# The D term of a selective scan: from matmuls on TensorE to a ScalarE write into the accumulator bank, with the convolution and the filler moved between slots

## The chip, the core and the metric

The kernel runs on one core of one Trainium2 chip. Its time is the device time of one execution in microseconds (us). Before the change the median of three executions was 8080.22 us. A profile is one execution recorded by the hardware profiler. In it PE is TensorE (PEld its weight loads), DVE is VectorE, ACT is ScalarE, POOL is GpSimd and SP is the queue that issues most DMAs.

## The reference, cut to what matters

The input has shape (4, 512, 64, 64): 4 batches, 512 channels, 4096 positions. Layer 0 is group norm, LayerNorm over channels, a Mamba block applied to four chunks of 128 channels with shared weights, a skip, a second LayerNorm and a 512 x 512 projection. Layer 1 is group norm and a linear attention with 8 heads. Each layer is added to its input. For a chunk x of shape (L, 128) the Mamba block computes

```python
xi, z = split(x @ in_proj_w.T)               # 256 inner channels each
xc = silu(causal_conv4(xi) + conv_b)
dt, Bs, Cs = split(xc @ x_proj_w.T)          # 8, 16 and 16 columns
dt = softplus(dt @ dt_proj_w.T + dt_proj_b)
h  = exp(dt * A) * h + (dt * xc) * Bs        # for each channel and 16 states, along L
y  = sum_over_states(h * Cs) + xc * D_param  # the last product is the D term
out = (y * silu(z)) @ out_proj_w.T + skip_scale * x
```

The change concerns `xc * D_param`, and the places at which the next chunk's `causal_conv4` and `z` are computed.

## The kernel before

**Steps and slots.** One step handles one batch b, one tile t of 512 positions and one chunk c of 128 channels: 4 x 8 x 4 = 128 steps. A step has 16 slots (`SLOTS`), 2048 slots in all. Slots 0 to 7 belong to inner channels 0 to 127 (e = 0), slots 8 to 15 to inner channels 128 to 255 (e = 1). Two slots together handle one group of 4 states; each slot does half of it. All emission is written out by hand under a manual schedule, so every engine executes its instructions in the order in which the Python code emits them.

**What a slot holds** (`slot`, L659). VectorE runs two scans (L673), called scan(s,0) and scan(s,1) here for slot s. Each scan takes its decay factors from a PSUM bank dA and its inputs from bx. ScalarE writes each dA bank with an exponential (`decay`, L642); there are three such banks, so it runs at most three scans ahead: decay(k), with k = 2s + i within the step, is queued behind scan number k - 3 and what that slot emitted before it. GpSimd makes bx two slots ahead (`drive`, L651, operation L655). After an odd slot it also stores the last state (L683) and multiplies the last quarter of the positions by C (L684). VectorE multiplies the other three quarters by C in `product` (L696), which is called product(s) here. It reads C from a single PSUM bank, c_all.

**Where C comes from.** `c_row` (L636) is one bf16 matmul that spreads the C rows of one group over the partitions. It is emitted inside `product` of an odd slot, when the bank has been read for the last time. c_all(s), for an even s, is the matmul that slot s's product reads. Behind it TensorE gets the fold of the group just finished (`fold_states`, L702): four matmuls of 32 columns each that run side by side and add the group's states into PSUM bank y. There is one bank for y. Because `AWAY = (3, 10)`, in which wide VectorE operations may follow the scans, product(s) runs after the first scan of slot s + 1, except for s = 4 and s = 11, whose products run at the end of their own slot. So slot 4 holds product(3), then one scan, then product(4).

**What else is emitted in each slot** (`after`, inside the loop over s from L1046). Pieces of the step's own bookkeeping have fixed slots:

- slot 0: `take_y` of the step before (e = 1), a ScalarE copy of bank y; slot 8: the same for this step (e = 0). It overwrites xc in `xz` with y.
- slots 1 and 9: the product with the gate on GpSimd; slot 2: `time_banks` (L544), two matmuls into two work banks; slot 3: `time_steps` (L551), the softplus on ScalarE that empties them, between two loads of activation tables; slot 4: dt times xc on GpSimd and `out_proj` (L724); slot 6: `with_skip`; slot 10: silu of the step after next, again between two table loads.
- slots 3, 5, 6, 7, 8, 9: one piece each of `inputs` (L512) of the step after next: two convolution taps, two taps, two taps, two taps, gate matmul, gate matmul. Each bank is copied out by ScalarE one slot later.

Everything else is filler that comes from three queues (`ahead`, `late`, `rest`): the LayerNorms (wide VectorE operations of 2.26 us only in slots 3 and 10), the projection, and the attention of the batch before. A filler piece is begun if there is credit for TensorE work (counted in fp32 matmuls of 512 columns) and if `room` finds fewer than `limit[0]` fillers holding a bank. There are three work banks (`ps_w`) for all of these.

**The D term.** At the first fold of each half step, bank y is started by `diagonal`: four matmuls of 32 x 32, side by side, of `dg` (D on a diagonal) with xc. The same helper starts the bank of `out_proj` with the skip scale.

The records of all matmuls stand at one line of the profile, L124, since one helper issues them.

## Time and profile before

| quantity | value |
|---|---|
| executions before (median, lowest, highest) | 8080.22, 8074.53, 8089.37 us |
| profiled execution, its own time | 8087.92 us |
| its span, first to last instruction | 8086.2 us |
| scans (L673) | 4096, mean 1267 ns (3584 of them), 1206 ns (512 of them) |
| products (L696) | 2048, mean 931 ns |
| exponentials (L647) | 4096, mean 688 ns |
| D packs (y<-xz,dg) | 2048 records, two to a matmul, 340.4 us busy |
| table loads | 1283 ns each |
| mean granted TensorE clock | 0.888 |

A row of the profile gives line, engine, operation, result and operands, shapes and count, and then the busy time and mean duration. In a timeline row the first number is the start in us, the second the duration of the rows merged in it. A bracket at its end tells how long the engine had been idle before the row and what ended that wait. In the view of waits a row gives who waited for whom, the total in us, how often, and the longest. Idle time of an engine is worth removing only if that engine sets the end.

### The profile page before, as it was taken

How to read it: one execution, taken by the hardware profiler on the slowest of the kernel's cores; microseconds unless marked ns; L12 is line 12 of the kernel's file. 1: busy time of each engine (PE TensorE's matmuls, PEld its weight loads, DVE VectorE, ACT ScalarE, POOL GpSimd, SP SyncE). 2: the span in 40 equal slices, each digit the busy share in tenths (PEclk: the TensorE clock that was granted, in tenths of full speed). 3: DMA queues.
4: the chain of work that ended last, by engine and by line, in shares of the span. 5: the costliest groups of instructions: out<-in, count | busy, mean ns of one | idle time of the engine just before them, and what ended most of it. 6: DMA issues, size and time to landing. Idle time of an engine off the chain costs nothing.

```text
span 8086.2 us, 92449 instructions
## 1 busy us (share of the span) xinstructions
PE 6471.4 (80%) x24800; PEld 2115.5 (26%) x24800; DVE 7113.0 (88%) x6815; ACT 5514.5 (68%) x8289; POOL 6890.3 (85%) x4597
## 2 busy tenths in 40 slices
PE   5677777667788878888788888888788888888599
PEld 1111111112222222322222222332222222322144
DVE  5999999999999999899999999999999999998600
ACT  4667777777767777677776767667777777776421
POOL 4999999999989989899998989888999999889600
PEclk8787888788899989898899999899889999999699
DMA  5666666666666666676666666667666666676402
GB/s 160 166 166 160 156 147 153 157 157 166 167 167 156 162 153 156 168 188 176 169 155 164 166 165 155 155 171 187 163 158 160 156 157 152 150 194 176 110 32 89
DMA packets 829199, 1265.98 MB, mean 157 GB/s; under 512 B 183912, under 2 KB 317560, under 8 KB 816384
## 3 DMA queue, kind: packets, MB, share of 16 engines
q1 hardware_dynamic: 804736, 1222.32, 59.7%
q0 software_dynamic: 16896, 33.56, 2.4%
q10 hardware_dynamic: 7040, 4.20, 0.2%
q8 instruction: 194, 3.18, 0.2%
q14 instruction: 333, 2.73, 0.1%
HBM read 1052.78 MB, written 206.57 MB: 156 GB/s over the span
## 4 chain that ended last, share of the span: by engine, by line
DVE 22%; PE 19%; DMA 17%; POOL 14%; issue 10%; ACT 9%; SPq 8%; POOLq 0%; DVEq 0%; ACTq 0%
DVE h L673 14%; POOL bx L655 10%; DMA d_all<-d_rows 9%; DVE h L696 7%; PE pq L124 5%; SPq L622 5%; DMA b_all<-b_rows 4%; ACT dA L647 3%; PE pc L124 3%; PE pr L124 3%; SPq L572 3%; PE y L124 3%; POOL h L684 2%; PE pp L124 1%; DMA c_sb<-c_rows 1%
## 5 line engine op out<-in xcount | busy, mean ns | idle before, releaser
L655 POOL TENSOR_TENSOR bx<-d_all,b_all 128x1024 f32<-128x1024 f32 x2048 | 4817.4, 2371 | 66.9 <-DVE h L673 51.5
L673 DVE TENSOR_TENSOR_SCAN h<-dA,st,bx 128x512 f32<-128x512 f32 x3584 | 4420.5, 1267 | 80.6 <-ACT dA L647 75.4
L647 ACT ACTIVATE dA<-d_all,a_t 128x512 f32<-128x512 f32 x4096 | 2780.4, 688 | 1764.2 <-DVE h L673 1727.5
L696 DVE TENSOR_TENSOR h<-h,c_all 128x768 f32<-128x768 f32 x2048 | 1906.7, 931 | 307.5 <-PE c_all L124 298.2
L124 PE MATMUL y<-h,fold 128*32 128x512 f32 x8192 | 1280.6, 701 | 160.5 <-POOL h L684 156.1
L684 POOL TENSOR_TENSOR h<-h,c_sb 128x512 f32<-128x512 f32 x1024 | 1299.3, 1269 | 121.4 <-DMA c_sb<-c_rows 33.5
L124 PE MATMUL pc<-xn,w_cv 128*128 128x512 f32 x2048 | 1078.8, 662 | 178.2 <-DVE xn L410 116.7
L124 PE MATMUL c_all<-parts,sel 128*128 128x384 bf16 x1024 | 368.3, 360 | 1058.5 <-DVE h L696 1056.1
L124 PE MATMUL pq<-w_qk,xa 128*128 128x512 f32 x2048 | 990.7, 615 | 1.9 <-ACT xa L348 1.9
L673 DVE TENSOR_TENSOR_SCAN h<-dA,bx 128x512 f32<-128x512 f32 x512 | 601.2, 1206 | 58.8 <-ACT dA L647 54.6
L124 PEld LDWEIGHTS pc<-xn,w_cv 128*128 128x128 f32 x2048 | 395.9, 204 | 807.7 <-issue 445.6
L124 PEld LDWEIGHTS <-sel 128*128 128x128 bf16 x1280 | 127.5, 100 | 1724.4 <-DVE h L696 1495.6
L683 POOL COPY st<-h 128x4 f32<-128x4 f32 x1024 | 206.9, 202 | 425.2 <-DVE h L673 382.2
L124 PEld LDWEIGHTS pq<-w_qk,xa 128*128 128x128 f32 x2048 | 402.8, 199 | 468.7 <-issue 446.2
L124 PE MATMUL pr<-xb,m 128*128 128x512 f32 x1024 | 500.4, 626 | 24.8 <-DMA xb<-x 16.5
L124 PE MATMUL pp<-xn,w_pr 128*128 128x512 f32 x1024 | 487.6, 602 | 3.8 <-DVE xn L410 3.8
L124 PEld LDWEIGHTS y<-h,fold 128*32 128x32 f32 x8192 | 170.9, 114 | 743.6 <-issue 281.0
L124 PE MATMUL y<-xz,dg 32*32 32x512 f32 x2048 | 340.4, 741 | 0.0
L720 POOL TENSOR_TENSOR xz<-xz 128x512 f32<-128x512 f32 x256 | 325.4, 1271 | 2.7 <-ACT xz L717 2.7
L561 POOL TENSOR_TENSOR dt<-dt,xz 128x1024 f32<-128x1024 f32 x128 | 302.2, 2361 | 25.5 <-ACT dt L553 25.5
L124 PE MATMUL pd<-xz,w_xp 128*128 128x512 f32 x512 | 311.6, 740 | 7.8 <-ACT xz L987 7.8
L771 ACT ACTIVATE kq<-pq 128x512 f32<-128x512 f32 x256 | 150.6, 588 | 232.6 <-PE pq L124 230.5
(169 smaller groups left out, 6063.9 us busy)
## 6 DMA issues: line engine op xcount, KB each, us to landing
d_all<-d_rows SPq DMA_DIRECT2D x2048, 256.0 KB, 6.6
b_all<-b_rows SPq DMA_DIRECT2D x4096, 64.0 KB, 2.2
d_rows<-dt SPq DMA_DIRECT2D x256, 512.0 KB, 3.7
c_sb<-c_rows SPq DMA_DIRECT2D x4096, 16.0 KB, 1.9
xs<-in_x_dram SPq DMA_DIRECT2D x32, 1024.0 KB, 5.8
xn<-in_x_dram SPq DMA_DIRECT2D x32, 1024.0 KB, 5.7
xr<-in_x_dram POOLq DMA_DIRECT2D x32, 1024.0 KB, 11.2
x<-xr SPq DMA_DIRECT2D x32, 1024.0 KB, 4.3
```

The source lines that it names most:

```text
L124: nc.tensor.matmul(out_, lhsT, rhs, **how)
L561: nc.gpsimd.tensor_tensor(f["both"][:, 1], f["both"][:, 0], f["xz"][:, 0], ALU.mult)
L572: nc.sync.dma_start(d[k * BLK : (k + 1) * BLK, v], src)
L622: nc.sync.dma_start(dst[k * BLK : (k + 1) * BLK, :], rows_[q * KS + k, :].partition_broadcast(BLK))
L647: nc.scalar.activation(dAs[k], fs[n]["d_all", e][:, 0, j, :], AF.Exp, scale=a_t[:, e, j, q : q + 1])
L655: nc.gpsimd.tensor_tensor(bxs[g], fs[n]["d_all", e][:, 1, jj * 2 : jj * 2 + 2, :], bc(b_all[g // JJ], 2), ALU.mult)
L673: nc.vector.tensor_tensor_scan(h[:, j, :], dAs.pop(2 * g + i), bxs[g][:, i, :], 0.0 if t == 0 else st[:, c, e, q, j : j + 1], ALU.mult, AL ...
L683: nc.gpsimd.tensor_copy(st[:, c, e, q, :], h[:, :, T - 1])
L684: nc.gpsimd.tensor_tensor(h[:, :, CUT:], h[:, :, CUT:], bc(c_sb.pop(g // JJ), NJ), ALU.mult)
L696: nc.vector.tensor_tensor(own, own, bc(c_all[g // JJ], 2), ALU.mult)
L720: nc.gpsimd.tensor_tensor(f["xz"][:, 1, e, :], f["xz"][:, 1, e, :], f["xz"][:, 0, e, :], ALU.mult)
L771: nc.scalar.activation(qk[i], pq, AF.Relu)
```

## The change

The D term is no longer computed by matmuls. `start_y`, called in slots 0 and 8 right after `take_y`, has ScalarE write xc times D into bank y, and all folds add to what is there (none has the start flag). One matmul at the beginning of the kernel (`y_first`) writes bank y once. `diagonal` goes away with `dg`; the start of `out_proj` does the same as before.

The first four pieces of `inputs` move from slots 3, 5, 6 and 7 to slots 5, 6, 7 and 8, and the two gate matmuls, in slots 8 and 9 before, are one piece in slot 9. The limit on fillers was 1 in slots 1 to 5 and 2 otherwise; it becomes 0 in slot 3, 1 in slots 1, 2, 4, 5, 8 and 9, and 2 otherwise. The credit for TensorE work is 3.4 a slot, 3.5 before.

```diff
-    def diagonal(out_, w, rhs):
-
-        for k in range(P // BLK):
-            r = slice(k * BLK, (k + 1) * BLK)
-            mm(out_[r, :], w[r, :], rhs[r, :], abreast=P // BLK, start=True, stop=False)
...
-    dg = const.tile([P, NH, BLK], F32, tag="dg", name="dg")
-    for e in range(NH):
-        nc.vector.tensor_scalar(dg[:, e, :], fold, dpar[:, e : e + 1], None, ALU.mult)
...
             later(1, lambda e=e, pz=pz: nc.scalar.copy(xz[:, 1, e, :], pz))
-            yield
...
         n, e, q, _ = place(g)
-        if q == 0:
-            ys[n, e] = ps_y.tile([P, T], F32, tag="y", name=f"y_{n}_{e}")
-            diagonal(ys[n, e], dg[:, e, :], fs[n]["xz"][:, 0, e, :])
         h = hs.pop(g // JJ)
         for j in range(NJ):
             mm(
                 ys[n, e][j * BLK : (j + 1) * BLK, :], fold, h[:, j, :],
-                start=False, stop=(q == NQ - 1), abreast=NJ,
+                start=False, stop=(q == NQ - 1), abreast=NJ, skip_group_check=True,
             )
+
+    def start_y(n, e):
+
+        ys[n, e] = ps_y.tile([P, T], F32, tag="y", name=f"y_{n}_{e}")
+        nc.scalar.activation(
+            ys[n, e], fs[n]["xz"][:, 0, e, :], AF.Copy, scale=dpar[:, e : e + 1]
+        )
...
+    y_first = ps_y.tile([P, T], F32, tag="y", name="y_first")
+    mm(y_first, ones.to_broadcast([P, P]), w_pr[:, 0, :], start=True, stop=True)
...
-                    if s == 0 and before is not None:
-                        take_y(before, n - 1, 1)
+                    if s == 0:
+                        if before is not None:
+                            take_y(before, n - 1, 1)
+                        start_y(n, 0)
                     if s == SLOTS // 2:
                         take_y(f, n, 0)
+                        start_y(n, 1)
...
-                    if s in (3, 5, 6, 7, 8, 9):
+                    if s in (5, 6, 7, 8, 9):
                         next(front, None)
...
-                    limit[0] = 1 if 0 < s < 6 else 2
-                    credit = min(credit + 3.5 - (work["mm"] - seen), 2.6)
+                    limit[0] = 0 if s == 3 else 1 if s in (1, 2, 4, 5, 8, 9) else 2
+                    credit = min(credit + 3.4 - (work["mm"] - seen), 2.6)
```

## The prediction

> **What bounds the kernel now.** First the page: engine shares, then the busy digits in 40 slices.

> ```profile
> span 8086.2 us, 92449 instructions
> ...
> PE 6471.4 (80%) x24800; PEld 2115.5 (26%) x24800; DVE 7113.0 (88%) x6815; ACT 5514.5 (68%) x8289; POOL 6890.3 (85%) x4597
> ...
> DVE  5999999999999999899999999999999999998600
> ```

> VectorE is full up to slice 37 and then empty: there is a main stage and a tail. I cut the span at the first and the last scan (120.30 and 7611.85 us) and asked for the busy time of PE, weight load, DVE, ACT and POOL in each stretch:

> ```profile
> 120.30:7611.85 7491.55, 5983.84 (x23179) 1894.06 (x23179) 7049.89 (x6656) 5378.42 (x8079) 6874.63 (x4576) 0.89 0.66 163
> 7611.85:8086.20 474.35, 435.61 (x1508) 199.20 (x1508) 26.30 (x74) 102.80 (x166) 5.59 (x6) 0.92 0.17 58
> ```

> In the main stage DVE is busy 7049.9 of 7491.6 us. The change takes nothing from DVE there, so it can win only from its 441.7 us of idle time. The view of waits, DVE alone, names that idle time:

> ```profile
> DVE h L696 <- PE c_all L124: 298.2, 165, 6.0
> ...
> DVE h L673 <- ACT dA L647: 130.1, 64, 46.7
> ...
> DVE h L673 <- POOL bx L655: 6.8, 13, 1.3
> ```

> The products (L696) wait for the C bank that TensorE fills, the scans (L673) for ScalarE's exponentials. Sorting these waits by slot (scans are counted in order, two to a slot) gives: slot 4, C bank, **207.4 us in 94 of 128 steps**; slot 12, exponentials, 62.2 in 42; slot 7, C bank, 52.2 in 36; slot 5, exponentials, 19.0 in 18; slots 15, 9 and 1, C bank, 18.0, 10.8 and 8.0; the start, 46.7 once. Slot 4 is special because product(3) and product(4) both run in it, with one scan between, so the C bank must be refilled within 1.23 us instead of two scans and more. One such place in the timeline:

> ```profile
> 3053.01 1.88 PE L124 MATMUL pq<-w_qk,xa 128*128 128x512 f32 x4
> ...
> 3054.56 1.28 ACT L1066 ACT_TABLE_LOAD   x1
> 3054.92 0.92 DVE L696 TENSOR_TENSOR h<-h,c_all 128x768 f32<-128x768 f32 x1
> ...
> 3055.86 1.26 ACT L553 ACTIVATE dt<-pt,dtb 128x512 f32<-128x512 f32 x2
> 3056.60 1.99 PE L124 MATMUL pc<-xn,w_cv 128*128 128x512 f32 x4 [1.71 <-ACT dt L553]
> ...
> 3058.42 1.88 PE L124 MATMUL pq<-w_qk,xa 128*128 128x512 f32 x4
> ...
> 3060.14 0.33 PE L124 MATMUL c_all<-parts,sel 128*128 128x384 bf16 x1
> ...
> 3060.50 0.95 DVE L696 TENSOR_TENSOR h<-h,c_all 128x768 f32<-128x768 f32 x1 [3.47 <-PE c_all L124]
> ```

> The convolution of slot 3 finds all three work banks taken and waits 1.71 us for the softplus to free one. The filler's second half stands behind it and c_all behind both, so DVE loses 3.47 us.

> [...] the eight records of a D pack start 7 ns apart, and the next pack starts 0.99 us after it (3024.22 to 3025.21). [...] The load is 1283 ns here, but the next instruction starts 20 ns after it (3054.56 + 1.28 to 3055.86)[...].

> **The change part by part.** One unit is an fp32 matmul over 512 columns: two records, 0.43 us apart. With gaps, 10.2 units between two c_alls took 9.21 us, 0.90 a unit. The instruction order of both kernels gives the units queued ahead of each c_all.

> *D term.* TensorE loses 256 packs of 1 unit (0.99 us each, 253 us of PE) and gets one matmul at the start. ScalarE gets 256 activations; nearest row the exponential, also from SBUF into PSUM with a scale operand: 0.688 us, 176 us of ACT. At slots 0 and 8 no scan is waiting on ACT (no such wait above): decay and queued work there are 0.8 + 2.1 and 0.8 + 1.4 us against 5.5 that DVE has, so 0 on the path. The fold of slot 2 waits for this write, some 2.5 us after it is due to be ready; above nothing, up to 0.5 us x 128 if take_y itself comes late; I take 0. DMA counts are the same on every queue; the SP and POOL orders lose and gain nothing but filler positions.

> *Slot 3 emptied.* Work between c_all(2) and c_all(4) falls from 6.74 units to 2.98 in the mean (pack 1.0, taps 1.97, fillers 0.8), and nothing there waits for softplus. In before, steps with about 5 units waited 0.4 us, with 9 units 3.2. After: 88 steps of 124 have 2 or 3 units, 24 have 4, 12 have 6. At 0.05, 0.2 and 1.1 us that leaves 22 us of 207.4: **-185**.

> *What is late next: slot 5.* The wait at slot 4 covered ScalarE's softplus (two loads and two activations, 2 x 1.283 + 2 x 0.687 = 3.94 us, plus filler work queued in slot 3). From the end of scan(3,1) to scan(5,1) DVE has three scans and two products, 3 x 1.23 + 2 x 0.93 = 5.55 us (2.26 more with a wide LayerNorm operation); ScalarE needs that block and 1.5 us for two exponentials and handoffs. Subtracting step by step for before gives 59 us without the slot-4 wait and 23 with it; measured 19.0. For after's order the same sum is 79 us in 54 steps, about 72 with what is left at slot 4: **+53**.

> *Slot 12.* Silu is a block of 1.283 + 1.911 + 1.283 = 4.48 us; both gate copies (0.58 each) now stand before it where one did. The same subtraction gives 59.7 us in 42 steps for before (measured 62.2 in 42) and 79.2 in 69 for after: **+18**. Here is one of before's, with ACT the cause:

> ```profile
> 3025.76 1.91 ACT L987 ACTIVATE xz<-xz 128x2048 f32<-128x2048 f32 x1
> 3027.69 1.28 ACT L1088 ACT_TABLE_LOAD   x1
> ...
> 3029.71 2.46 DVE L673 TENSOR_TENSOR_SCAN h<-dA,st,bx 128x512 f32<-128x512 f32 x2 [1.05 <-ACT dA L647]
> ```

> *Denser slots 5 to 9.* Work before c_all(6), (8), (10) goes 8.01 to 8.62, 6.24 to 6.84, 5.56 to 6.36 units. By units alone before's waits would make slot 7 83 us. But c_all(4) is now early, which gives TensorE 0.75 us more, and slot 5 gives some: between 14 and 83, I take 40 (**-12**). Slot 9 by units 29, I take 25 (**+14**). Slot 11 had no wait; 15 steps have filler behind the gate matmuls and no wide operation: 15 x 0.5 = **+8**. Slot 15 goes 18 to 22 (**+4**).

> *Unknown.* The gate matmuls now wait in 71 of 122 steps for a bank copied out in the same slot 9, so silu may start late: 0 to 30, I take +5. POOL needs 53.7 us a step, DVE will have 57.8 instead of 58.5: +5 (0 to 20). The tail has 474.5 units in both kernels: 0. A higher granted clock with less PE work could give up to 20 back; I take 0.

> Sum: -185 + 53 + 18 - 12 + 14 + 8 + 4 + 5 + 5 = **-90 us**. The profiled execution took 8087.92 (span 8086.2), 7.7 above the median of three, 8080.22. So 7998 on its own scale, 7990 on that of the median.

> **Rivals.** *ScalarE takes all of it.* If slots 5, 6 and 12 together grow by 140 instead of 71, and slot 7 stays at 52, the sum is about -10 to -40: 8050. For it: ACT gets 176 us of work, and both its blocks were near their limit. Against: the subtraction met both measured sums within 4 us. *More is won.* Slot 4 goes to 0, the softplus stall hides slot 7's (14), the clock rises: -185 - 22 - 26 - 20 makes 7925 to 7940. *Slower: bank ping-pong at slot 9.* TensorE's gate matmuls wait for ScalarE's copy of the second convolution bank, silu waits for them, and the scans of slot 12 for silu. It decides if the second gate matmul ends more than 0.7 us past decay(24), the last exponential ahead of the copies, in nearly every step; at 1.5 us x 128 = 192 us it turns -90 into +100: 8180. Against: the copy runs at about 1.4 us after scan(9,1), the two matmuls end near 3.3, and ACT reaches their copies at 4.2. For: c_all(10) already came up to 2.3 us late at the tenth decile. *It doesn't do what it says* (fillers begun in slot 2 fill slot 3 as before): the order shows 2.98 units, so only the clock could spoil it; -30, 8050.

> **How the numbers follow.** My forecast (-60 to -130) 0.60; more won 0.11; small gain, by ScalarE or otherwise (-17 to -60) 0.17; no change 0.04; slower 0.08. A measurement of this kernel tells about 0.2%, 16 us, from none. Faster 0.88, same 0.04, slower 0.08. The range takes in the bounds of slots 4, 5 and 7: 7930 to 8060.

> **What would show it.** Right: no D packs (y<-xz,dg) on PE and an ACT row into y of 256 near 0.69 us; DVE waits for c_all near 120 instead of 298; DVE waits for dA up from 130 to about 200, at slots 5 and 12; main stage near 7402; tail 474 as before. Wrong: waits for c_all at slot 4 above 60 us, dA waits above 270, or DVE waiting for bx above 30.

## The result: slower by 1.5%, and the profile after

The changed kernel takes **8202.32 us** in the median of four executions (8201.15 to 8207.79), against 8081.74 for the kernel before in four (8074.53 to 8089.37). The ratio is 1.015, with a 95% interval of 1.0133 to 1.0168. The forecast of 7990 us had the wrong sign: 120 us were lost where 90 should have been won. The profiled execution took 8201.15 us, so its trace can be read as it stands. One of the four executions of e2 below, at 12759.63 us, is far from every other run and is left out of its time.

From the page of the changed kernel, the span, the busy times and the granted TensorE clock in 40 slices:

```profile
span 8199.4 us, 89045 instructions
...
PE 6331.9 (77%) x22754; PEld 2094.7 (26%) x22754; DVE 7122.3 (87%) x6813; ACT 5668.9 (69%) x8545; POOL 6891.6 (84%) x4597
...
PEclk8777777777888888898888889889888989889799
```

The same clock line on the page of the kernel before:

```profile
PEclk8787888788899989898899999899889999999699
```

TensorE has less to do (6331.9 us busy for 6471.4) and its clock is lower: 0.853 in the mean for 0.888. The prediction did not read this line; of the clock it had only the mean of the main stage, 0.89. Its unit of 0.90 us comes from stretches between two c_alls in which the granted clock was full (1.00).

The cut at the first and the last scan, in the columns of the table before (span, then busy PE, PEld, DVE, ACT, POOL, clock, DMA share, GB/s):

```profile
121.13:7725.12 7603.99, 5843.40 (x21131) 1872.56 (x21131) 7059.56 (x6656) 5532.75 (x8335) 6876.00 (x4576) 0.85 0.65 161
7725.12:8199.40 474.28, 435.40 (x1508) 199.21 (x1508) 26.31 (x75) 102.80 (x166) 5.60 (x6) 0.92 0.17 58
```

All of it lies in the main stage: 7604.0 us for 7491.6, **+112.4**. DVE's work there grew by only 9.7, so the rest is idle time of DVE. The tail is 474.3, as before. DVE's waits after (the scans are L662 now, the products L685):

```profile
DVE h L662 <- ACT dA L636: 251.0, 141, 46.1
DVE h L685 <- PE c_all L124: 231.6, 123, 9.8
...
DVE h L662 <- POOL bx L644: 15.2, 18, 3.1
```

The waits for c_all fell by 67 us, where 178 were forecast; those for dA rose by 121, where about 70 were. Others grew too: the scans' for bx by 8, and those of other DVE operations, for banks of the attention, the projection and the LayerNorms, by 29. With DVE's extra work the sum is +102 of the 112.4; the other 10 are in gaps too short for this view. By slot, in the prediction's manner:

| wait of DVE, us | before | forecast | after |
|---|---|---|---|
| slot 4, c_all | 207 | 22 | **7** |
| slot 5, dA | 19 | 72 | 83 |
| slot 6, dA | 1 | not named | 18 |
| slot 7, c_all | 52 | 40 | **139** |
| slot 9, c_all | 11 | 25 | 15 |
| slot 12, dA | 62 | 80 | 92 |
| slot 15, c_all | 18 | 22 | **66** |

Slot 4 went as planned. Two C banks that should have been little touched came late instead: c_all(6), which slot 7's product reads, and c_all(14).

**Where slot 7's time went.** The timeline of the changed kernel, PE only, over slots 2 to 7 of one step (start, duration, operation, idle before):

```profile
3202.70 2.08 PE L124 MATMUL pt<-dt,w_dt 32*128 32x512 f32 x4
3209.03 0.50 PE L124 MATMUL c_all<-parts,sel 128*128 128x384 bf16 x1 [4.25 <-DVE h L685]
3209.46 1.94 PE L124 MATMUL y<-h,fold 128*32 128x512 f32 x8
3211.33 1.93 PE L124 MATMUL po<-xn,skd 32*32 32x512 f32 x8
...
3220.11 0.33 PE L124 MATMUL c_all<-parts,sel 128*128 128x384 bf16 x1
3220.37 1.06 PE L124 MATMUL y<-h,fold 128*32 128x512 f32 x8
```

And the windows of the same stretch:

```profile
3206.00:3209.40 3.40, 0.37 (x1) 0.10 (x1) 3.40 (x4) 3.37 (x4) 3.38 (x2) 0.50 0.55 113
3209.40:3212.80 3.40, 3.40 (x17) 0.40 (x16) 3.30 (x4) 3.39 (x6) 3.40 (x3) 0.50 0.35 99
3212.80:3216.20 3.40, 3.40 (x16) 1.04 (x12) 3.40 (x4) 1.09 (x2) 3.32 (x4) 0.86 0.88 331
3216.20:3222.00 5.80, 5.80 (x24) 2.19 (x21) 3.31 (x4) 4.29 (x7) 4.34 (x3) 1.00 0.19 35
```

In slot 3, now emptied, TensorE stands still for 4.25 us and waits for the product that frees the C bank. The clock is at 0.50. Then the densest work of the step begins, and for the first 3.4 us of it TensorE is busy without a gap at half clock; only in the third row does the clock come up. The fold pack shows it in one number: from 3209.46 the next pack starts 1.87 us later, from 3220.37, at full clock, 0.99. So c_all(6) starts 11.1 us after c_all(4), and slot 7's product waits 2.49 us for it:

```profile
3220.47 0.95 DVE L685 TENSOR_TENSOR h<-h,c_all 128x768 f32<-128x768 f32 x1 [2.49 <-PE c_all L124]
```

The mean over all steps says the same: from c_all(4) to c_all(6), 8.69 units took 10.13 us after and 8.07 units 7.88 us before. In steps with about 10 units it was about 11.0 and 9.4 us.

The granted clock by slot follows the idle time. TensorE stood idle right ahead of c_all(4) for 0.14 us in the mean before, for over 2 us in 4 of 128 steps; after, 3.22 us, over 2 us in 91. In slots 4 and 5 the clock went from 0.83 and 0.99 to 0.59 and 0.74. Over the whole execution the time at half clock went from 1806 to 2404 us.

**Where slot 15's time went.** This is in part something else. A filler matmul, `pr<-xb,m`, stands ahead of c_all(14) in four steps and waits there for the DMA that brings its input. From the view of PE's waits, and from the worst of these steps:

```profile
PE pr L124 <- DMA xb<-x: 26.9, 4, 8.4
...
3861.06 3.75 PE L124 MATMUL pr<-xb,m 128*128 128x512 f32 x4 [8.39 <-DMA xb<-x]
...
3870.66 0.96 DVE L685 TENSOR_TENSOR h<-h,c_all 128x768 f32<-128x768 f32 x1 [9.84 <-PE c_all L124]
```

The products of slot 15 wait 29 of their 66 us in these four steps. In the kernel before such a wait stood three times ahead of c_all(0), and never ahead of c_all(14). The filler's place moved with the change.

### The profile page after: what moved, and what is told of

The parts are those of the page before. It is cut to its first block, busy times and chain, and to the rows that moved or that the text cites. A ratio compares the mean times of both kernels' runs of the same rounds, so it can differ in the third digit from the quotient of the medians.

```text
span 8199.4 us, 89045 instructions
## 1 busy us (share of the span) xinstructions
PE 6331.9 (77%) x22754; PEld 2094.7 (26%) x22754; DVE 7122.3 (87%) x6813; ACT 5668.9 (69%) x8545; POOL 6891.6 (84%) x4597
## 4 chain that ended last, share of the span: by engine, by line
PE 24%; DVE 20%; DMA 17%; POOL 12%; ACT 11%; issue 8%; SPq 7%; POOLq 0%; DVEq 0%; ACTq 0%
DVE h L662 12%; POOL bx L644 9%; DMA d_all<-d_rows 8%; DVE h L685 6%; PE pq L124 5%; SPq L611 4%; ACT dA L636 4%; PE y L124 4%; DMA b_all<-b_rows 3%; PE pc L124 3%; PE pr L124 3%; PE po L124 3%; SPq L561 2%; PE pp L124 2%; POOL h L673 2%
## 5 line engine op out<-in xcount | busy, mean ns | idle before, releaser
L644 POOL TENSOR_TENSOR bx<-d_all,b_all 128x1024 f32<-128x1024 f32 x2048 | 4817.2, 2377 | 100.6 <-DVE h L662 85.4
L662 DVE TENSOR_TENSOR_SCAN h<-dA,st,bx 128x512 f32<-128x512 f32 x3584 | 4429.5, 1268 | 198.5 <-ACT dA L636 185.0
L685 DVE TENSOR_TENSOR h<-h,c_all 128x768 f32<-128x768 f32 x2048 | 1910.4, 933 | 251.7 <-PE c_all L124 231.6
L124 PE MATMUL c_all<-parts,sel 128*128 128x384 bf16 x1024 | 385.6, 377 | 1467.9 <-DVE h L685 1446.5
L124 PE MATMUL y<-h,fold 128*32 128x512 f32 x8192 | 1350.8, 737 | 203.5 <-POOL h L673 194.4
L673 POOL TENSOR_TENSOR h<-h,c_sb 128x512 f32<-128x512 f32 x1024 | 1300.2, 1270 | 171.6 <-DMA c_sb<-c_rows 78.7
L124 PE MATMUL pq<-w_qk,xa 128*128 128x512 f32 x2048 | 1010.6, 628 | 1.6 <-ACT xa L338 1.6
L124 PE MATMUL pc<-xn,w_cv 128*128 128x512 f32 x2048 | 996.0, 615 | 9.0 <-ACT xn L406 4.6
L124 PEld LDWEIGHTS <-sel 128*128 128x128 bf16 x1280 | 127.4, 100 | 2158.6 <-DVE h L685 1995.4
L662 DVE TENSOR_TENSOR_SCAN h<-dA,bx 128x512 f32<-128x512 f32 x512 | 602.2, 1208 | 70.8 <-ACT dA L636 66.0
L124 PEld LDWEIGHTS pq<-w_qk,xa 128*128 128x128 f32 x2048 | 409.7, 203 | 481.6 <-issue 461.7
L124 PE MATMUL pr<-xb,m 128*128 128x512 f32 x1024 | 502.0, 631 | 30.7 <-DMA xb<-x 26.9
L124 PEld LDWEIGHTS pc<-xn,w_cv 128*128 128x128 f32 x2048 | 366.0, 191 | 611.5 <-issue 574.1
L124 PE MATMUL pp<-xn,w_pr 128*128 128x512 f32 x1024 | 484.3, 601 | 3.8 <-DVE xn L400 3.8
L124 PEld LDWEIGHTS y<-h,fold 128*32 128x32 f32 x8192 | 173.9, 117 | 601.8 <-POOL h L673 329.6
L124 PE MATMUL pd<-xz,w_xp 128*128 128x512 f32 x512 | 306.2, 729 | 7.8 <-ACT xz L985 7.8
L124 PE MATMUL po<-xz,w_op 128*128 128x512 f32 x512 | 286.2, 684 | 2.1 <-POOL xz L713 2.1
```

The lines of the kernel that those rows point to most:

```text
L124: nc.tensor.matmul(out_, lhsT, rhs, **how)
L644: nc.gpsimd.tensor_tensor(bxs[g], fs[n]["d_all", e][:, 1, jj * 2 : jj * 2 + 2, :], bc(b_all[g // JJ], 2), ALU.mult)
L662: nc.vector.tensor_tensor_scan(h[:, j, :], dAs.pop(2 * g + i), bxs[g][:, i, :], 0.0 if t == 0 else st[:, c, e, q, j : j + 1], ALU.mult, AL ...
L673: nc.gpsimd.tensor_tensor(h[:, :, CUT:], h[:, :, CUT:], bc(c_sb.pop(g // JJ), NJ), ALU.mult)
L685: nc.vector.tensor_tensor(own, own, bc(c_all[g // JJ], 2), ALU.mult)
```

## The experiments

Three theories stood after the result. **Clock**: the work is as predicted, but TensorE begins it at half clock, because the stretch before it is empty. **Density**: there is simply too much between c_all(4) and c_all(6), and a gap before it doesn't matter. **ScalarE**: the writes of the D term make the exponentials late. The kernel before ran beside each group, at 8087.02, 8086.64 and 8087.42 us; all ratios are to it, with their 95% intervals. The changed kernel was not run again: differences from its 8202.32 us reach across groups, between which the kernel before differs by 5 us.

**e1_busy3: useless matmuls in slot 3.** At the end of slot 3 zero-weight matmuls add nothing to bank y, until 5 units stand between c_all(2) and c_all(4).

```diff
+    def keep_busy(n, e, units):
+        had = work["mm"] - since[0]          # since[0] is set in c_row
+        while had < units:
+            nc.tensor.matmul(ys[n, e], none.to_broadcast([P, P]), w_pr[:, 0, :],
+                start=False, stop=False, skip_group_check=True)
+            had += 1.0
...
+                    if s in {3: 5.0}:
+                        keep_busy(n, s // 8, {3: 5.0}[s])
```

> The changed kernel, with about 2.5 matmuls of zero weights per step added at the end of slot 3, as many as bring the TensorE work between c_all(2) and c_all(4) to 5 units. They add zero to bank y, need nothing that is late, and change nothing else. Clock theory (the emptied slots 3 and 4 leave TensorE idle, its clock falls to half, 0.589 granted in slot 4 and 0.741 in slot 5, and the 8.7 units up to c_all(6) take 10.03 us instead of about 8): the clock in slots 4 and 5 returns to 0.8 or more, the wait for c_all at slot 7 falls from 139 us to 60 or less, and the time from 8202 to 8090 to 8130. Density theory (slots 5 to 9 simply hold too much work): slot 7 keeps its 139 us, slot 4 may get worse, and the time is 8200 or more. ScalarE theory (the D writes make the exponentials late): no change, 8200.

8110.16 us, ratio 1.0027 (1.0016 to 1.0038): **92 us faster than the changed kernel by doing more**. The same step in its PE timeline, the added matmuls in the second row:

```profile
3176.83 2.08 PE L124 MATMUL pt<-dt,w_dt 32*128 32x512 f32 x4
3178.84 4.77 PE L134 MATMUL y<-w_pr,none 128*128 128x512 f32 x6
3183.44 0.33 PE L124 MATMUL c_all<-parts,sel 128*128 128x384 bf16 x1
3183.70 1.06 PE L124 MATMUL y<-h,fold 128*32 128x512 f32 x8
...
3192.35 0.33 PE L124 MATMUL c_all<-parts,sel 128*128 128x384 bf16 x1
```

The same work from c_all(4) to c_all(6) takes 8.9 us here and 11.1 above; in the mean over all steps 8.69 us for 10.13. The clock in slots 4 and 5 is back at 0.80 and 0.95, from 0.59 and 0.74. Over all steps slot 7's wait falls from 139 to 69 us, and slot 4's rises only from 7 to 44. Density alone would have kept slot 7 where it was. For slot 7 the clock theory stands, though the 69 us left are still more than the 52 of the kernel before.

**e2_dterm_only and e3_slots_only: each half of the change by itself.** e2 is the kernel before with `start_y` and `y_first` and without D packs; e3 is the kernel before with the moved pieces, the limits and the credit, and with its D packs.

```diff
e2
-            diagonal(ys[n, e], dg[:, e, :], fs[n]["xz"][:, 0, e, :])
+        start_y(n, e)     # in slots 0 and 8, as in the change
e3
-                    if s in (3, 5, 6, 7, 8, 9):
+                    if s in (5, 6, 7, 8, 9):
...
-                    limit[0] = 1 if 0 < s < 6 else 2
+                    limit[0] = 0 if s == 3 else 1 if s in (1, 2, 4, 5, 8, 9) else 2
```

> The kernel before with the D term on ScalarE alone; convolution, gate branch, limits and credit as before. Clock theory: slot 3 keeps its two taps and filler, so TensorE is idle little longer than before and the loss is small: 8060 to 8120, with the wait at slot 4 still above 150 us. ScalarE theory: 176 us of ScalarE work shows as waits for dA, and most of the loss of 120 us is here: 8170 or more. Density theory: one unit less in slots 2 and 10, so a little faster than before, 8040 to 8070.

> The kernel before with the moves alone: convolution in slots 5 to 8, gate branch in slot 9, no filler begun in slot 3, limits and credit of the changed kernel; the D term stays with TensorE, one unit each in slots 2 and 10. Clock theory: the pack of slot 2 fills a part of the gap only (3.98 units up to c_all(4) instead of 2.98), so most of the loss is here, with the clock of slot 4 between 0.59 and 0.83: 8110 to 8180. Density theory: all of the loss is here, 8200 or somewhat more, since TensorE has 256 units more. ScalarE theory: faster than before, 7990 to 8040.

e2 8145.77, 1.0075 (1.0055 to 1.0095); e3 8223.93, 1.017 (1.0155 to 1.0185). Both halves lose, and both by more than the clock theory had expected. Their losses, some 60 and 137 us, do not add up to the 120 of the change: removing the packs lost time with the slots as before, but e3, which keeps them with the slots moved, is no faster than the changed kernel (1.017 for 1.015, with intervals that overlap), so there their removal lost nothing. In e2 the loss is mainly slot 15's wait, 69 us for 18. Of the 69, 28 stand in three steps in which `pr<-xb,m` waits some 9 us for its input ahead of c_all(14). The granted clock in slots 11 to 13 is 0.80, 0.70 and 0.71, where it was 0.95, 0.81 and 0.77. In e3 slot 7 waits 140 us, as in the changed kernel, with slots 3 to 6 at a clock of 0.82, 0.73, 0.75 and 0.92. e3's time falls where density had put it. But from c_all(4) to c_all(6) it takes 10.12 us for 8.77 units at a clock of 0.83, and e8 below does as many in 8.93 at 0.95.

**e5_dterm_zero_pack: the D term on ScalarE, and a pack of zeros where the D pack stood.** It asks whether e2 lost to the ScalarE write or to the work that TensorE no longer has.

```diff
+        if q == 0:
+            for k in range(P // BLK):
+                r = slice(k * BLK, (k + 1) * BLK)
+                mm(ys[n, e][r, :], none[r, :].to_broadcast([BLK, BLK]), rhs[r, :],
+                    abreast=P // BLK, start=False, stop=False, skip_group_check=True)
```

> The D term on ScalarE, slots as before (e2), and a pack of four zero-weight matmuls on TensorE exactly where the D pack stood. TensorE then has the work of the kernel before, ScalarE 256 activations more. Clock theory: what e2 lost (62 us, of it 51 at slot 15, where the clock of slots 11 to 13 had gone from 0.946, 0.811, 0.770 to 0.803, 0.696, 0.714) comes back: 8080 to 8105, slot 15's wait for c_all near 20 us instead of 69. ScalarE theory (the activations themselves cost it): stays near 8149.

8083.79, ratio 0.9996 (0.9988 to 1.0005). The 256 writes cost nothing that can be measured, which ends the ScalarE theory. With zeros in the place of the packs, slot 15 is back at 16 us and the clock at 0.889, so e2's whole loss goes with the packs. It doesn't follow that it was all the clock's. A pack also counts in the credit by which fillers are begun, zeros or not, so e5 has its fillers where the kernel before has them, and no `pr<-xb,m` waits ahead of c_all(14). Of the 1025 stretches that the c_alls mark off, 1000 hold the same matmuls as before in e5, packs apart, and 702 in e2. Of the 51 us that e2 lost at slot 15, 28 are that filler's. The other 23 came with a lower clock, but no run parts the clock from the order of the fillers there.

**e4_busy_all and e6_busy3_10: the clock kept up elsewhere too.** Both are e1 with fills at more slots.

```diff
-                    if s in {3: 5.0}:
+                    if s in {1: 4.5, 3: 5.0, 11: 4.0, 13: 4.5}:     # e4
+                    if s in {3: 5.0, 10: 4.0}:                      # e6
```

> The changed kernel with zero-weight matmuls that fill the stretches before c_all(2), c_all(4), c_all(12) and c_all(14) to 4.5, 5, 4 and 4.5 units. Clock theory: granted clock above 0.92 in the mean, waits for c_all at slots 7 and 15 (139 and 66 us) down to 40 and 30: 8050 to 8110, below the version filled in slot 3 alone. Density theory: slower than the changed kernel, 8220 or more, since TensorE gets about 1000 matmuls more. ScalarE theory: 8200.

> The changed kernel with zero-weight matmuls in slot 3 (to 5 units, as e1) and in slot 10 (to 4 units up to c_all(12)). Clock theory: slots 11 to 13 rise from 0.889, 0.724, 0.721 to 0.9, 0.8, 0.77 or more, slot 15's wait falls from 69 to 20 to 35 us: 8060 to 8080, the first variant at or below the kernel before. Density theory: as e1 or slower, 8110 to 8130.

e4 took 8232.47, 1.0185 (1.017 to 1.02), a miss. Its clock line shows what it got:

```profile
PEclk8888888888899999999999999999999999999899
```

The clock is 0.917, above both kernels, and slot 7 has 62 us. But the fills issued in slot 1 stand ahead of c_all(2), and those of slots 11 and 13 ahead of c_all(14), and those then come late: slot 3 waits 66 us (2 before), slot 15 122. The stretch before c_all(12) got no fill, unlike what had been expected: c_all(12) is emitted in slot 11 ahead of the fill, and the clock of slots 11 to 13 stayed at 0.88, 0.71 and 0.74. Fill has to stand where nobody waits behind it. e6 took 8093.83, 1.0009 (1.0002 to 1.0015), 16 us less than e1 but short of the 8060 to 8080 expected. The clock in slots 11 to 13 is back (0.97, 0.89, 0.81), but slot 15 falls only from 69 to 59. So in the changed kernel most of slot 15's wait has another cause than the clock. In 28 of the 59 us it is `pr<-xb,m` again, which waits for its input in the same four steps; no run moved it. The rest stays open.

**e7_limit1: the changed kernel with one filler allowed in slot 3.**

```diff
-                    limit[0] = 0 if s == 3 else 1 if s in (1, 2, 4, 5, 8, 9) else 2
+                    limit[0] = 1 if s in (1, 2, 3, 4, 5, 8, 9) else 2
```

> The changed kernel with one edit undone: slots 1 to 5 again let one filler be begun, slot 3 too. Clock theory: useful filler closes part of the gap (3.97 units up to c_all(4) in the mean instead of 2.98, but a third of the steps stays at 2), so the clock of slot 4 rises a little and slot 7 falls from 139 to about 100; some fillers wait again for the softplus and bring 30 to 50 us back at slot 4: 8150 to 8200. If the ban on fillers were the whole cause: near 8090.

8122.9, 1.005 (1.0033 to 1.0067): this one part of the change was worth about 79 us of the loss, more than expected. TensorE's idle time ahead of c_all(4) goes from 3.22 to 1.02 us and slot 7 to 97, with slot 4 at 40. Slot 12 rises to 134. The gain isn't the clock's alone: slot 5 falls from 83 to 25, and slot 15 from 66 to 43, since no `pr<-xb,m` waits ahead of c_all(14) in this order.

**e9_busy3_gates: e1 with the two gate matmuls apart, one in slot 8 and one in slot 9.** It asks whether slot 12's growth comes from both copies standing ahead of silu.

```diff
             later(1, lambda e=e, pz=pz: nc.scalar.copy(xz[:, 1, e, :], pz))
+            yield
...
+                    if s == 8:
+                        next(front, None)
```

> The changed kernel with slot 3 filled to 5 units (e1, 8110), and the two gate matmuls one in slot 8 behind the last taps and one in slot 9, so that only one of their two copies stands ahead of silu in slot 10. Theory of the silu block: the wait for dA at slot 12 falls from 92 us to 60 to 70 (62 in the kernel before), and the time from 8110 to 8075 to 8090. Rival (the two copies cost nothing; slot 12 waits because TensorE is late with the gate matmuls): slot 12 keeps 80 us or more, and 8105 to 8120.

8104.77, 1.0022 (1.0013 to 1.0031): a miss, no gain. Slot 12 waits 89 us, as with the copies together (92). The trace shows a part of the reason: the copy that moved now stands ahead of decay(24), which starts 0.25 us later for it, so the table load ahead of silu comes only 0.23 us earlier (4.90 us after the start of scan(10,0), 5.13 in e1), where the copy itself takes 0.58. The rival's reason isn't seen: ScalarE waits for the gate matmuls for 3.8 us in the whole run. For the change as it is, the subtraction came near: 79 worked out, 92 measured. What else holds slot 12 is open.

**e8_before_limit0 and e10_before_shift: the gain of slot 4 without its price.** e8 is the kernel before, D packs and slots as they were, with no filler begun in slots 2 and 3. e10 also begins no attention filler in slots 4, 5, 7 and 8.

```diff
-                    limit[0] = 1 if 0 < s < 6 else 2
+                    limit[0] = 0 if s in (2, 3) else 1 if 0 < s < 6 else 2
...
+                        if queue is rest and s in (4, 5, 7, 8) and kind not in ("more", "free", "wait"):   # e10 alone
+                            continue
```

> The kernel before with one edit: no filler begun in slots 2 and 3. The D pack and the two convolution taps stay, so nearly every step has 5 units up to c_all(4) (5.35 in the mean, 6.79 before) and TensorE is never idle for long there. Clock theory: the clock of slots 4 and 5 stays at 0.8 and 0.95 or more, the wait at slot 4 falls from 207 to 20 to 70 us, slot 5 gains 40 and slot 7 some 20 us: 7970 to 8030, below the kernel before. Rival (less filler in slots 2 and 3 is enough to lose the clock, as in the changed kernel): 8100 or more.

> As e8 (the kernel before, no filler begun in slots 2 and 3), and the attention's fillers not begun in slots 4, 5, 7 and 8 either, so that they go to slots 0, 1 and 9 to 15. Units up to c_all(6) 8.39 in the mean instead of 8.77, up to c_all(14) 7.11 instead of 6.90; the tail keeps its 474.5. Density theory for what is left in e8 (84 us at slot 7, 66 at slot 9): some 40 us fewer there, 8020 to 8050. Clock theory alone (the clock in slots 5 to 9 is at 0.94 to 0.99 already): no change, 8055 to 8070. Rival: what is removed at slots 7 and 9 comes back at slots 11 and 15: 8060 to 8100.

e8 took **8063.61 us** in the median of 12, ratio 0.9973 (0.9965 to 0.9982), the fastest of all. DVE's waits in it:

```profile
DVE h L696 <- PE c_all L124: 210.0, 164, 5.0
DVE h L673 <- ACT dA L647: 114.5, 91, 5.3
DVE h L673 <- POOL bx L655: 56.6, 16, 45.4
```

(The 45.4 is the wait at the start of the main stage, which stood with dA before.) Slot 4 falls from 207 to 41 with the fillers gone from ahead of c_all(4). The convolution stays in slot 3 and keeps TensorE at work: 5.35 units, 0.40 us of idle time, and a clock of 0.81 and 0.96 in slots 4 and 5. But slot 7 takes 84, slot 9 66 and slot 5 65 us, which are 32, 55 and 46 more than before: 133 of the 166 come back at once. It missed its expectation of 7970 to 8030. e10 took 8069.63, 0.9978 (0.9969 to 0.9988), and wins nothing over e8. Thinner slots 4 to 8 left slot 7 at 77 and slot 9 at 63, and slot 5 rose to 74.

## Why the prediction was wrong, point by point

- **Slot 4: right**, and a little more: 207 to 7, forecast 22.
- **Slot 5: right.** 83 measured, 72 forecast. Slot 6's +17, by the same softplus block, was left out.
- **Slot 12: right in direction**, 92 for 80, and 70 steps for 69. Parting the copies didn't bring it back (e9).
- **D term on ScalarE at 0 on the path: right** (e5). The prediction took 0.688 us for the operation; the view of tile y, ACT (count, shortest, median and longest in ns), has:

```profile
L704 ACT ACTIVATE y<-xz,dpar x256: 671/692/694, 124.1 to 7705.5; 128x512 f32<-128x512 f32 x128
```

Whether this write needs `y_first` ahead of it was not shown: every run with the write has it.

- **D term taken from TensorE at 0: wrong by itself.** The 256 packs were booked as harmless to lose. Alone this lost about 60 us (e2), and zeros in the same place gave all of it back (e5): 28 us of it were a moved filler's, and the rest went with a lower clock. With the slots moved no such loss is seen (e3). The size of a pack was right, one unit of 0.99 us. Its eight records aren't all 7 ns apart, as the prediction has it: they start in two groups of four, with 0.43 us between the groups.
- **Slot 7: the step that failed most.** From 83 by units the prediction took off 0.75 us of earlier start and came to 40: measured 139. The units were right (8.62 forecast, 8.69 found). What failed is 0.90 us a unit, measured at full clock and carried into slots where the change itself took the clock to 0.59: there it was 1.17 us a unit (10.13 for 8.69). The clock isn't all of the miss: with the clock mostly back slot 7 still waits 69 us (e1), and 84 in e8 with 8.77 units at 0.95, so about 30 to 45 of the 99 us over the forecast go with the denser stretch. The edit that brings c_all(4) earlier is the one that emptied TensorE ahead of it.
- **"A higher granted clock with less PE work could give up to 20 back; I take 0": wrong in sign.** The 20 us were the author's estimate, with no trace behind them. Half-clock time rose by 598 us, from 1806 to 2404. Apart from a rival (below), this was the only place where the prediction let the clock move.
- **Slot 15: 66 for 22.** 29 us are `pr<-xb,m` waiting for its input in four steps. The prediction mentioned moved filler positions and put no price on them. Restoring the clock gives back only 10 of 69 us (e6). The rest isn't settled.
- **Slots 9 and 11**: 15 and 2.5 us for 25 and 8. Small.
- **The tail at 0: right.**
- **The rival on the losing side**, the bank ping-pong at slot 9, named 8180 and did not happen: in the changed kernel ScalarE waits for the gate matmuls for 0.9 us in the whole run. That the end came out near its number is chance. The rival "only the clock could spoil it" named the clock, but not where it would strike, and had the wrong size: 60 us over the forecast where 212 were found.
- **The rival "more is won"** is written as a sum from -185, which leaves out the +95 of the other terms. With them it is -158, or 7922 us, near the 7925 stated.

Sizes: of the 120 us, filling slot 3 gives back 92 (e1), and allowing a filler there 79 (e7). These are two ways at one loss and don't add up. In e1 slots 5, 6, 7, 12 and 15 together still stand 150 us above the kernel before, and slot 4 163 below it: even with the clock mostly restored the wait was moved rather than removed. DVE's waits for c_all are 93 us below the kernel before there and those for dA 90 above; the 23 us by which e1 stays behind lie in its other waits (some 20) and in short gaps (6).

## What to carry to other kernels

A stretch of TensorE that stands ahead of its densest work was not free to be emptied here: the first 3.4 us after it ran at half clock, and the wait removed in front came back behind. Read the clock line and the granted clock by stage before a time per matmul is carried into a changed order, and ask whether the edit makes a gap of a few microseconds. See also which fillers the edit moves: one that waits for its input is dear where a matmul behind it is awaited (`pr<-xb,m` ahead of c_all(14), 29 us in four steps). Move the work that blocks the awaited matmul, but leave enough other work ahead of it, as e8 does; fill ahead of a matmul that someone waited for cost more than the clock gave (e4).

## What the runs showed of the hardware

| window | next window at the other clock | of these, before and after |
|---|---|---|
| full clock, PE busy below 40% | 1996 of 1996 | 339 of 339 |
| full clock, PE busy 60% or more | 89 of 16416 | 14 of 2621 |
| half clock, PE busy below 70% | 0 of 2377 | 0 of 489 |
| half clock, PE busy 90% or more | 2584 of 2854 | 447 of 512 |

Between these shares both happened. So some 2 us without work in one window (60% of 3.41) were enough in these traces to lose the clock, and it came back only after a window busy 70% or more.

Matmuls with zero weights kept the clock up here: the mean was 0.889 in e5 with them and 0.858 in e2 without. In the traces of e1, e4, e5, e6 and e9, 215 windows at full clock had PE busy 60% or more with the zero matmuls and below 40% without them; none was followed by half clock.
